# Turning normalised tokens by DMA through DRAM and VectorE 32x32 blocks in a fused attention and gate kernel

## The chip, the cores and the metric

The kernel runs on one core of a Trainium2 chip. The metric is the device time of one execution in microseconds (us); lower is better. Times are medians of several runs of the same program. A second source is one execution recorded by the hardware profiler; its span runs from the first instruction to the last.

The engines of the core: TensorE (PE in the profile; PEld is its weight load), VectorE (DVE), ScalarE (ACT), GpSimd (POOL), and SyncE (SP), which here only issues DMAs. Each engine works through its own instructions in order, and so does each queue of DMA issues: an instruction that waits holds up all behind it on its engine.

## The reference

Eight batches of 1024 tokens with 512 features, 16 heads of 32 features, all in float32:

```python
xn = layernorm(x)                      # mean and variance over the 512 features
q, k, v = (split_heads(xn @ W.T + b) for W, b in ((Wq, bq), (Wk, bk), (Wv, bv)))
scores = q @ k.T / sqrt(32)
im = arange(1024) % 256
scores = where(im[:, None] >= im[None, :], scores, -1e30)
s = merge_heads(softmax(scores) @ v) @ Wo.T + bo
y = clip((xn @ sign(ffn_weights).T) * scale + bias, -100, 100)
out = x + s * (y * sigmoid(y))
```

The mask depends on the positions modulo 256 only. The attention result and the gate both start from the layer-normalised tokens `xn`, and both need `xn` with features on partitions, because a matmul sums over partitions.

## The kernel before, in words

**Tiling.** The tokens of a batch are cut into eight tiles of 128 (`tokens`, `load_x`). A tile holds 32 tokens from each of the four windows of 256, so that the mask becomes causal between tiles and only the tiles on the diagonal need a mask inside. Four tiles make a half (512 tokens). The features are four chunks of 128 (`NC`), and one chunk is one group of four heads.

**The loop.** The loop from line 1109 goes over 8 batches x 4 groups x 9 steps. In each step:

- `probs_quad` makes scores with keys on partitions, four heads side by side, in one PSUM tile of four banks (the "t" quad, L592, L603, L614). ScalarE takes the exponential out of it (L627).
- `attend_quad` multiplies the step before's probabilities with the values (L640).
- `maxima_quad` makes scores of the next group with queries on partitions (the "s" quad, L525), and VectorE takes their row maxima (L537). They become the shifts of the next group's exponentials (`shift_parts`, L551, `shift_rows`).
- Between these, TensorE gets products of other parts: the query, key and value projections, the gate product (`gate_work`, L456, followed by VectorE's L433, L434, L442 and a store, L445), and the output product of the batch before (`output_work`, L739, L740, L741, a store, L742).

The pool `ps_q` has one buffer, so the two quads of a step use the same four banks: the s quad waits until the exponential has read the t quad, and the next t quad waits until the maxima have been read.

**The planner.** Matmuls are emitted by hand in this order. `Beside` holds a list of `Work` items with a cost in us. `fill` takes items from it until their costs reach what the step wants: some 1.2 us between the t and the s quad, and 2.35 us or more after the s quad, or the group's even share. The order of the items is in strings (`OPENING` for batch 0, `STEADY`, `CLOSING` for the last batch), in which each word is one block. A free item (cost 0), such as an operation of VectorE or a DMA, hangs on a block by its number (`link`). It is emitted when that block comes up, if its `ready` says so. Otherwise it is put off. Free items that come up before the s quad are kept until the maxima have been emitted.

**Normalising the next batch.** The words `N0` and `N1` stand for the two halves of the next batch. Per tile there are: the statistics on VectorE (`stats`, L292, L293; marked late, at most two are emitted at the end of a step), a few small operations per half on GpSimd (`scale`), the normalised tile in place on ScalarE (`normalise`, L316), and the turn (L320 to L331): four TensorE transposes of 128x128 (L328) into a PSUM bank and a ScalarE copy to `xnT` (L329). The turn costs 0.5 in the planner and is marked `turn`, which keeps it to certain places in a step. Batch 0's own tiles are normalised and turned ahead of the loop, by the same function.

**The DMA queue.** Nearly all transfers are issued from SP: x tiles (`load_x`, L137), the gate's stores to DRAM and reloads (L445, L729), the second load of x for the residual (`xb`, L733), and the stores of the output (L742). The pool `xpool` has five buffers for x tiles. The next batch's tiles 0 to 3 are loaded during group 0. The loads of tiles 5, 6 and 7 are linked so that each comes after the turn of tile 0, 1 and 2.

Of the kernel before, what the change touches and what calls it, by code (L numbers as in the profile page):

```python
# [9 lines left out]
F32 = mybir.dt.float32  # L10
# [6 lines left out]
P = 128  # L17
B = 8
L = 1024
D = 512  # L20
# [4 lines left out]
NC = D // P  # L25
NH = P // DK
HALF = 512
# [10 lines left out]
MT = P // NW  # L38
# [35 lines left out]
def tile_gated_window_attention(  # L74
# [16 lines left out]
    nc = tc.nc  # L91
    PSUM = bass.MemoryType.PSUM

    def pool(name, bufs, **kw):
        return ctx.enter_context(tc.tile_pool(name=name, bufs=bufs, **kw))
# [4 lines left out]
    seq = pool("seq", 2)  # L100
# [7 lines left out]
    rows_p = pool("rows", 1)  # L108
    small = pool("small", 4)
    spill = pool("spill", 2, space=bass.MemoryType.DRAM)  # L110
    ps_q = pool("ps_q", 1, space=PSUM)
    ps_a = pool("ps_a", 2, space=PSUM)
    ps_t = pool("ps_t", 2, space=PSUM)
# [7 lines left out]
    def bank(name, dtype=F32, n=512):  # L121
        return ps_t.tile([P, n], dtype, tag="bank", name=name)
# [8 lines left out]
    xt = {}  # L131
# [37 lines left out]
    for name, src in (("fscale", fscale), ("fbias", fbias), ("bo", bo)):  # L169
        t = const.tile([P, D], F32, name=f"{name}_r")  # L170
# [61 lines left out]
    wT, turned = {}, set()  # L232
# [46 lines left out]
        return [lambda c=c: turn(c) for c in range(NC)]  # L279


    xnT, scaled, normed = {}, set(), set()

    def norm_work(b, half):
        its = range(4 * half, 4 * half + 4)
        mv, rstd, shift_by = {}, {}, {}

        def stats(i, it):
            if i == 0:
                mv[0] = small.tile([P, 4, 2], F32, tag="mv", name=f"mv_{b}_{half}")  # L290
            st = small.tile([P, 6], F32, tag="st", name=f"st_{b}_{it}")
            nc.vector.bn_stats(st, xt[b, it])  # L292
            nc.vector.bn_aggr(mv[0][:, i, :], st)  # L293

        def scale(lo=0, hi=4):
            if lo == 0:
                rstd[0] = small.tile([P, 4], F32, tag="rstd", name=f"rstd_{b}_{half}")
            r = rstd[0][:, lo:hi]
            nc.gpsimd.tensor_scalar(r, mv[0][:, lo:hi, 1], EPS, None, ALU.add)
            nc.gpsimd.tensor_tensor(r, r, neg_half[:, lo:hi], ALU.pow)  # L300
            if b == 0:
                return
            shift_by[0] = small.tile([P, 4], F32, tag="nmr", name=f"nmr_{b}_{half}")
            scaled.add((b, half))
            nc.gpsimd.tensor_tensor(shift_by[0], mv[0][:, :, 0], rstd[0], ALU.mult)
            nc.gpsimd.tensor_scalar(shift_by[0], shift_by[0], -1.0, None, ALU.mult)

        def normalise(i, it):
            x = xt[b, it]
            normed.add((b, it))  # L310
            if b == 0:
                nc.vector.tensor_scalar(
                    x, x, mv[0][:, i, 0:1], rstd[0][:, i : i + 1], ALU.subtract, ALU.mult
                )
                return
            nc.scalar.activation(  # L316
                x, x, AF.Identity, bias=shift_by[0][:, i : i + 1], scale=rstd[0][:, i : i + 1]
            )

        def turn(i, it):  # L320
            if (b, half) not in xnT:
                xnT[b, half] = seq.tile([P, NC, HALF], F32, tag="xnT", name=f"xnT_{b}_{half}")
            turned.add((b, it))
            ps = bank(f"xnT_ps_{b}_{it}")
            x = xt.pop((b, it))
            normed.discard((b, it))
            for c in range(NC):
                nc.tensor.transpose(ps[:, c * P : (c + 1) * P], x[:, c * P : (c + 1) * P], ident)  # L328
            nc.scalar.copy(  # L329
                xnT[b, half][:, :, i * P : (i + 1) * P], ps.rearrange("p (c t) -> p c t", c=NC)  # L330
            )  # L331

        return (
            [lambda i=i, it=it: stats(i, it) for i, it in enumerate(its)],
            scale,
            [lambda i=i, it=it: normalise(i, it) for i, it in enumerate(its)],
            [lambda i=i, it=it: turn(i, it) for i, it in enumerate(its)],
        )

    def xn_cols(b, it):  # L340
# [39 lines left out]
    def values_work(b, it):  # L380
        def after(ps):

            vt[b, it] = vpool.tile([P, D], F32, tag="v", name=f"v_{b}_{it}")
            nc.scalar.copy(vt[b, it], ps)

        return product(
            f"v_ps_{b}_{it}",
            [(lambda c=c: (xn_cols(b, it)[:, c, :], wT["wv"][:, c, :])) for c in range(NC)],
            0.86,
            after,  # L390
            lambda: (b, it) in turned,
        )

    def heads_work(b, g, half, which):

        w, bias, into = {"q": ("wq", bq_c, qt), "k": ("wk", bk_c, kt)}[which]

        def after(ps):
            if (b, g) not in into:
                into[b, g] = qk.tile([P, L], F32, tag=which, name=f"{which}_{b}_{g}")  # L400
            nc.scalar.activation(  # L401
                into[b, g][:, half * HALF : (half + 1) * HALF], ps, AF.Identity,
                bias=bias[:, g : g + 1], scale=1.0,
            )

        return product(
            f"{which}_ps_{b}_{g}_{half}",
            [
                (lambda c=c: (wT[w][:, c, g * P : (g + 1) * P], xnT[b, half][:, c, :]))
                for c in range(NC)  # L410
            ],
            0.86,
            after,
            lambda: all((b, half * 4 + i) in turned for i in range(4)),
        )
# [423 lines left out]
    def link(i, fn, tail=False):  # L839
        links.append((i, fn, tail))  # L840

    def plan(b, g, text):
        for word in text.split():
            kind, number = word[0], word.strip("'")[1:]
            bb = b + word.count("'")
            i = len(blocks)
            if kind == "|":
                for block in blocks:
                    block.early = block.early or block.at == (b, g)
                continue  # L850
            if kind == "N":
                half = int(number)
                stats, scale, normalise, turn = norm_work(b + 1, half)
                for k in range(4):
                    done = lambda key=(b + 1, 4 * half + k): key in normed
                    there = lambda key=(b + 1, 4 * half + k): key in xt
                    link(
                        i - 5 + (2 + k // 2 if half else 0) + k // 2,
                        Work(0, stats[k], late=True, ready=there),
                    )  # L860
                    by = lambda key=(b + 1, half): key in scaled
                    link(i + half + max(1, k), Work(0, normalise[k], ready=by))
                    link(i + half + 2 + k, Work(0.5, turn[k], turn=True, ready=done))
                link(i - 2 + 2 * half, Work(0, scale, late=True, ready=there))
                continue
            if kind == "-":
                main = []
            elif kind in "qk":
                main = heads_work(bb, int(number[0]), int(number[1]), kind)
            elif kind == "V":  # L870
                main = values_work(bb, int(number))
            elif kind == "W":
                main = [Work(0.5, turn_weight("wo")[int(number)], turn=True)]
            elif kind == "R":
                spread, main = row_work()
                link(i - 3, spread)
            elif kind == "O":
                fetch, main = output_work(b - 1, int(number))
                link(i - 1, fetch)
            else:  # L880
                split, main, squash, finish = gate_work(bb, int(number), kind == "H")
                if split is not None:
                    link(i - 3, split)
                later = 1 if b in (0, B - 1) else 0
                link(i + 2 + later, squash)
                link(i + 3 + later, finish)
            blocks.append(Block((b, g), main))

    for b in range(B):
        for g in range(NC):  # L890
# [7 lines left out]
            elif g == 1:  # L898
                for k in range(4):

                    ready = lambda key=(b + 1, k - 1): key[1] < 0 or key in turned
# [121 lines left out]


    norms = [norm_work(0, half) for half in range(2)]

    warm = ps_a.tile([P, 512], F32, tag="av", name="warm")

    def idle_turns(n):
        for _ in range(n):  # L1030
            nc.tensor.transpose(warm[:, 0:P], ident, ident)

    idle_turns(36)
    stats, scale, normalise, turn = norms[0]
    key_turns, first_keys = turn_weight("wk"), heads_work(0, 0, 0, "k")
    first_keys = [w.split(0.43) for w in first_keys]
    stats[0]()
# [30 lines left out]
    stats, scale = norms[1][:2]  # L1068
# [40 lines left out]
    for s, (b, g, n) in enumerate(steps):  # L1109
# [4 lines left out]
        turn = {0: (b, g, 0), 7: (*nxt, 1) if nxt else None}.get(n)  # L1114
        add = {LAST[1] + 2: None if last else (b, g, 1), 2: (*old, 0) if old else None}.get(n)
        now, kept = side(b, g), []
# [87 lines left out]
    b, g = B - 1, NC - 1  # L1204
# [66 lines left out]
```

## Time and profile before

| what | value |
|---|---|
| median of 3 runs | 2215.35 us (2215.28 to 2217.46) |
| span of the profiled execution | 2213.6 us, so 1.75 us of the median lie outside the span |
| TensorE busy | 2182.9 us, granted clock 1.000 |
| GpSimd busy | 1325.6 us |
| VectorE busy | 1276.7 us |
| ScalarE busy | 876.0 us |
| DMA | 93.60 MB, 42 GB/s over the span |

A step of the loop takes 6.9 to 8.3 us, a group of nine 64 to 69 us, a batch some 268 us. Batch 0 and the start before it are slower in places, and the last batch has no next batch beside it. TensorE is busy nearly all the time; the other engines wait for it. The profile gives busy time per group of instructions, what each waited for, and single instructions in a window of the timeline. A row of a group reads: line, engine, operation, output and inputs with their shapes, count, then the busy time and the mean of one in ns, then the idle time of the engine just before them and what ended it.

### The profile page before, as it was taken

To read this page: it belongs to the slowest core of one execution; us is meant where nothing else is said; L and a number is where in the kernel's file an instruction comes from. 1 tells how busy PE (TensorE), PEld (TensorE's weight loads), DVE (VectorE), ACT (ScalarE), POOL (GpSimd) and SP (SyncE) were. 2 spreads that over 40 slices of the span, in tenths; PEclk is the share of its full clock that TensorE was granted. 3 is DMA by queue.
4 is the path that set the end of the run, shared out by engine and by line. 5 is a ranking of instruction groups with operands and counts; after the bars stand their busy time and mean duration, and the time that the engine had idled before them with its cause. 6 is when DMAs were issued, how large, how long until landed. Compare 5 with 4: busy or idle time off the path is not lost. (4 is left out here: it accounts for less than half of the span.)

```text
span 2213.6 us, 57362 instructions
## 1 busy us (share of the span) xinstructions
PE 2182.9 (99%) x26015; PEld 857.3 (39%) x26015; DVE 1276.7 (58%) x1635; ACT 876.0 (40%) x862; POOL 1325.6 (60%) x1198
## 2 busy tenths in 40 slices
PE   8999999999999999999999999999999999999998
PEld 4334333333333443333333333334333443333333
DVE  4556556665557655566555665565655665555564
ACT  2235433444344444344443443434443343333332
POOL 1356565666566656576556665556765666755562
PEclk9999999999999999999999999999999999999999
DMA  4001000121001210012000120002200111000113
GB/s 167 2 16 35 11 7 30 54 73 35 25 25 40 73 35 25 25 59 72 16 25 25 63 68 16 25 25 68 63 16 25 45 59 63 11 21 25 44 54 125
DMA packets 49676, 93.60 MB, mean 42 GB/s; under 512 B 5388, under 2 KB 5656, under 8 KB 49432
## 3 DMA queue, kind: packets, MB, share of 16 engines
q1 hardware_dynamic: 48728, 88.76, 12.1%
q8 instruction: 203, 3.33, 0.6%
q10 hardware_dynamic: 704, 1.18, 0.2%
q14 instruction: 41, 0.34, 0.0%
HBM read 56.37 MB, written 33.55 MB: 41 GB/s over the span
## 5 line engine op out<-in xcount | busy, mean ns | idle before, releaser
L659 POOL TENSOR_TENSOR p<-p,p 128x512 f32<-128x512 f32 x930 | 1096.3, 1209 | 395.2 <-ACT p L627 242.9
L537 DVE TENSOR_REDUCE pm<-s 128x4 f32<-128x2048 f32 (+3 forms) x384 | 664.0, 1750 | 588.6 <-PE s L525 586.7
L627 ACT ACTIVATE p<-t 128x2048 f32<-128x2048 f32 x288 | 540.9, 1878 | 839.3 <-PE t L614 764.0
L715 DVE RECIPROCAL aT<-aT 128x128 f32<-128x128 f32 x256 | 230.3, 928 | 214.9 <-ACT aT L676 214.9
L525 PE MATMUL s<-k,q 32*128 32x512 f32 (+3 forms) x3072 | 315.3, 504 | 1.1 <-ACT q L401 0.8
L640 PE MATMUL av<-p,v 128*32 128x512 f32 (+3 forms) x3072 | 307.4, 495 | 1.6 <-DVE aT L719 1.4
L614 PE MATMUL t<-q,k 32*128 32x512 f32 (+3 forms) x3072 | 306.1, 492 | 0.0
L358 PE MATMUL k_ps<-xnT,wkT 128*32 128x512 f32 (+3 forms) x2832 | 254.9, 477 | 1.7 <-ACT wkT L274 0.7
L358 PE MATMUL q_ps<-xnT,wqT 128*32 128x512 f32 (+2 forms) x2656 | 254.1, 497 | 1.7 <-ACT shift L572 0.8
L358 PE MATMUL v_ps<-wvT,xnT 128*32 128x512 f32 (+3 forms) x2728 | 254.8, 489 | 0.0
L358 PE MATMUL o_ps<-woT,aT 128*32 128x320 f32 (+2 forms) x2568 | 243.9, 503 | 1.5 <-ACT shift L572 0.8
L741 POOL TENSOR_TENSOR s<-s,xb 128x512 f32<-128x512 f32 x63 | 86.3, 1370 | 212.3 <-DVE s L740 210.2
L358 PEld LDWEIGHTS k_ps<-xnT,wkT 128*32 128x32 f32 x2832 | 83.7, 109 | 169.0 <-issue 138.3
L614 PEld LDWEIGHTS t<-q,k 32*128 32x128 f32 x3072 | 139.1, 185 | 25.8
L358 PEld LDWEIGHTS q_ps<-xnT,wqT 128*32 128x32 f32 x2656 | 78.9, 109 | 174.0 <-issue 151.6
L640 PEld LDWEIGHTS av<-p,v 128*32 128x32 f32 x3072 | 70.3, 108 | 195.9 <-issue 163.4
L358 PEld LDWEIGHTS v_ps<-wvT,xnT 128*32 128x32 f32 x2728 | 79.2, 109 | 168.6 <-issue 143.5
L456 PE MATMUL y_ps<-fwT,x 128*128 128x512 f32 x464 | 135.5, 418 | 1.7 <-ACT k L401 1.3
L525 PEld LDWEIGHTS s<-k,q 32*128 32x128 f32 x3072 | 117.0, 184 | 52.0 <-ACT p L627 42.2
L358 PEld LDWEIGHTS o_ps<-woT,aT 128*32 128x32 f32 x2568 | 76.1, 109 | 151.4 <-issue 133.1
L429 POOL TENSOR_TENSOR x<-xnT,x 128x512 fp32r<-128x512 f32 x58 | 74.1, 1277 | 100.0 <-ACT x L428 100.0
L435 POOL TENSOR_SCALAR y<-y 128x512 f32<-128x512 f32 x64 | 39.6, 619 | 153.1 <-DVE y L434 101.3
(96 smaller groups left out, 1475.8 us busy)
## 6 DMA issues: line engine op xcount, KB each, us to landing
g<-t SPq DMA_DIRECT2D x64, 256.0 KB, 2.0
gb<-g SPq DMA_DIRECT2D x64, 256.0 KB, 2.9
xb<-in_L_attn_x_dram SPq DMA_DIRECT2D x64, 256.0 KB, 3.1
out_dram<-s SPq DMA_DIRECT2D x63, 256.0 KB, 2.5
x<-in_L_attn_x_dram SPq DMA_DIRECT2D x62, 256.0 KB, 3.1
wq_st<-in_L_attn_Wq_dram SPq DMA_DIRECT2D x2, 512.0 KB, 5.1
wv_st<-in_L_attn_Wv_dram SPq DMA_DIRECT2D x2, 512.0 KB
fw_st<-in_L_ffn_weights_dram SPq DMA_DIRECT2D x2, 512.0 KB, 9.7
```

The costliest lines, as they stand in the source:

```text
L358: nc.tensor.matmul(hold[0][cols, lo:hi], lhsT=lhsT[:, cols], rhs=rhs[:, lo:hi], start=(i == 0 and lo == 0), stop=(i == n - 1), skip_group_ ...
L429: nc.gpsimd.tensor_tensor(part[1], src, part[0].bitcast(F32), ALU.subtract)
L435: nc.gpsimd.tensor_scalar(y[0], y[0], MAX_VAL, -MAX_VAL, ALU.min, ALU.max)
L456: nc.tensor.matmul(hold[0], lhsT=part[i][:, c, :], rhs=wT["fw"][:, c, :], start=(i == 0 and c == 0), stop=(i == 1 and c == NC - 1),)
L525: nc.tensor.matmul(sc[:, h, at : at + w], lhsT=qt[b, g][head_rows(h), i * P : (i + 1) * P], rhs=kt[b, g][head_rows(h), lo:hi], start=(at = ...
L537: nc.vector.tensor_reduce(pm[:, 0 if lo == 0 else 1, i, :], sc[:, :, at : at + w], AX.X, ALU.max)
L614: nc.tensor.matmul(sc[:, h, at : at + w], lhsT=kt[b, g][head_rows(h), j * P : (j + 1) * P], rhs=qt[b, g][head_rows(h), q0 : q0 + w], start ...
L627: nc.scalar.activation(pt[:, :, :width], sc[:, :, :width], AF.Exp, scale=SCALE)
L640: nc.tensor.matmul(av[b, g, f][head_rows(h), lo : lo + w], lhsT=vt[b, j][:, g * P + h * DK : g * P + (h + 1) * DK], rhs=pts[b, g, n][:, h, ...
L659: nc.gpsimd.tensor_tensor(t[:, hs, lo : lo + w], t[:, hs, lo : lo + w], p[:, hs, at : at + w], ALU.add)
L715: nc.vector.reciprocal(r, r)
L741: nc.gpsimd.tensor_tensor(s, s, xr, ALU.add)
```

## The change

From the second batch on, the four transposes and the copy of a turn are replaced by two steps. Both are free items.

- `shuffle`, as soon as a tile is normalised: SP stores the tile of 128 tokens x 512 features (256 KB) to DRAM. Four DMAs load it back into the same SBUF tile, each one filling 32 partitions. Partition block j gets, for each chunk c and token block t, the 32 features of block j in chunk c: 32 partitions x 16 pieces of 32 features (128 bytes), 64 KB a load. The first load waits until the store has landed.
- `turn_blocks`: one VectorE transpose of 128 x 512, which turns each block of 32x32 in place of its own, from the x tile into `xnT`.

With blocks moved by the DMA and each block turned by VectorE, `xnT` holds what the TensorE transposes gave. The shuffle hangs on the block on which the normalise hangs. The block transpose hangs on block i + 4 + k for tile k of its half; the TensorE turn hung on i + half + 2 + k. A new pool `moved` has four DRAM buffers. Batch 0's own tiles are turned on TensorE as before.

For 7 batches of 8 tiles, 224 TensorE transposes and 56 ScalarE copies go; 56 stores, 224 loads and 56 VectorE transposes come.

```diff
@@ pools
     spill = pool("spill", 2, space=bass.MemoryType.DRAM)
+    moved = pool("moved", 4, space=bass.MemoryType.DRAM)
@@ norm_work(b, half)
+        def shuffle(i, it):
+            x = xt[b, it]
+            kept = moved.tile([P, D], F32, tag="xd", name=f"xd_{b}_{it}")
+            nc.sync.dma_start(kept, x)
+            from_rows = kept.rearrange("(t p) (c j f) -> j p c t f", p=MT, j=NH, f=MT)
+            for j in range(NH):
+                nc.sync.dma_start(
+                    x[j * MT : (j + 1) * MT, :].rearrange("p (c t f) -> p c t f", t=NH, f=MT),
+                    from_rows[j],
+                )
+            shuffled.add((b, it))
+
+        def turn_blocks(i, it):
+            if (b, half) not in xnT:
+                xnT[b, half] = seq.tile([P, NC, HALF], F32, tag="xnT", name=f"xnT_{b}_{half}")
+            turned.add((b, it))
+            x = xt.pop((b, it))
+            normed.discard((b, it))
+            nc.vector.transpose(xnT[b, half][:, :, i * P : (i + 1) * P], x)
@@ plan(b, g, text)
-                stats, scale, normalise, turn = norm_work(b + 1, half)
+                stats, scale, normalise, _, shuffle, turn = norm_work(b + 1, half)
@@
                     link(i + half + max(1, k), Work(0, normalise[k], ready=by))
-                    link(i + half + 2 + k, Work(0.5, turn[k], turn=True, ready=done))
+                    link(i + half + max(1, k), Work(0, shuffle[k], ready=done))
+                    there2 = lambda key=(b + 1, 4 * half + k): key in shuffled
+                    link(i + half + 4 - half + k, Work(0, turn[k], ready=there2))
```

More of the change, by code (lines that the diff above doesn't have):

```diff
@@ L279, in turn_weight @@
         return [lambda c=c: turn(c) for c in range(NC)]
-    xnT, scaled, normed = {}, set(), set()
+    xnT, scaled, normed, shuffled = {}, set(), set(), set()
     def norm_work(b, half):
@@ L337, in norm_work @@
             [lambda i=i, it=it: turn(i, it) for i, it in enumerate(its)],
+            [lambda i=i, it=it: shuffle(i, it) for i, it in enumerate(its)],
+            [lambda i=i, it=it: turn_blocks(i, it) for i, it in enumerate(its)],
         )
@@ L1033, in tile_gated_window_attention @@
     idle_turns(36)
-    stats, scale, normalise, turn = norms[0]
+    stats, scale, normalise, turn = norms[0][:4]
     key_turns, first_keys = turn_weight("wk"), heads_work(0, 0, 0, "k")
```

## The prediction

> **What bounds the kernel now.** I read, in this order, the page's first part (engines), the waits, the costliest groups with shapes kept apart, the DMA issues, then the timeline of batch 4, the middle of five near-equal batches. 0.2% (4.4 us) is about what a measurement of this kernel can tell from no change.
>
> The page:
> ```profile
> span 2213.6 us, 57362 instructions
> PE 2182.9 (99%) x26015; PEld 857.3 (39%) x26015; DVE 1276.7 (58%) x1635; ACT 876.0 (40%) x862; POOL 1325.6 (60%) x1198
> ```
> The waits, engine by engine:
> ```profile
> ACT p L627 <- PE t L614: 764.0, 261, 6.5
> DVE pm L537 <- PE s L525: 586.7, 195, 11.0
> PEld s L525 <- ACT p L627: 42.2, 97, 0.8
> PEld L592 <- DVE pm L537: 29.1, 62, 1.8
> ```
> TensorE is busy throughout and ACT and DVE wait for it. But a busy PE does not set every step: with one four-bank PSUM buffer for both quads, a step is the loop t quad, exp (L627, 1878 ns), s quad, maxima (L537, 2287 ns), next t. PE's waits inside that loop are short because products fill them. The distance from one exp to the next, read off the timeline, shows what filling costs (groups, batches and steps count from 0): in group 0 of batch 7, with nothing of a next batch beside it, the nine steps are 6.89, 6.92, 6.95, 7.03, 7.12, 7.37, 7.21, 7.09, 7.17 us. I take these as the bare loop. Batch 4's groups last 67.0, 68.8, 66.4 and 66.0 us against that row's 63.7.
>
> Of what the change touches, groups (count | busy, mean ns | idle before):
> ```profile
> L328 PE MATMUL xnT_ps<-ident,x 128*128 128x128 f32 x256 | 41.5, 286 | 3.3 <-DVE x L312 1.6 <-DVE y L434 1.0 <-ACT xnT L329 0.4
> L329 ACT COPY xnT<-xnT_ps 128x512 f32<-128x512 f32 x64 | 37.2, 585 | 86.0 <-PE xnT_ps L328 86.0
> L434 DVE TENSOR_TENSOR y<-y_ps,fbias_r 128x512 f32<-128x512 f32 x64 | 44.3, 692 | 2.6
> L442 DVE SCALAR_TENSOR_TENSOR t<-t,y 128x512 f32<-128x512 f32 x64 | 53.4, 836 | 0.0
> L292 DVE BATCH_NORM_STATS2 st<-x 128x6 f32<-128x512 f32 x64 | 43.1, 674 | 8.8 <-DMA x<-in_L_attn_x_dram 8.8
> ```
> The last row matters: statistics stand in DVE's order before a maximum, so a late x stalls the loop. The one place where DVE, not PE, already sets the step, batch 4, group 2, step 0 (start, duration):
> ```profile
> 1286.32 0.94 DVE L715 RECIPROCAL aT<-aT 128x128 f32<-128x128 f32 x1
> 1287.18 0.70 DVE L442 SCALAR_TENSOR_TENSOR t<-t,y 128x512 f32<-128x512 f32 x1
> 1287.81 1.75 DVE L715 RECIPROCAL aT<-aT 128x128 f32<-128x128 f32 x2
> 1289.58 2.29 DVE L537 TENSOR_REDUCE pm<-s 128x4 f32<-128x2048 f32 x1
> ```
> The reduction follows two reciprocals with no gap. And the queue, SP, in DMA rows (KB each, us to landing) and timeline:
> ```profile
> g<-t SPq DMA_DIRECT2D x64, 256.0 KB, 2.0
> x<-in_L_attn_x_dram SPq DMA_DIRECT2D x62, 256.0 KB, 3.1
> ```
> ```profile
> 1259.98 1.36 SPq L137 DMA_DIRECT2D x<-in_L_attn_x_dram  x2
> 1287.91 0.33 SPq L445 DMA_DIRECT2D g<-t  x1
> 1293.83 0.54 SPq L733 DMA_DIRECT2D xb<-in_L_attn_x_dram  x1
> ```
>
> **The change, part by part.**
>
> *1. TensorE loses 56 of 64 turns.* A merged run of four transposes shows 0.65-0.66 us, and 0.59 us pass to PE's next instruction, so 56 turns are 33-36 us of PE time. What returns is limited by the bare loop. In batch 4 the turns fall in group 1's steps 5 to 8 (7.62+7.94+7.92+8.31 = 31.8 us; bare 28.8, room 3.0, turns 2.5) and group 2's steps 3 to 7 (37.6; bare 35.8, room 1.8): 2.5 + 1.8 = 4.3 us a batch. Batches 2 to 6 give 21.5, batch 1 about 3.8, batch 0 (crowded otherwise) 1.9: **-27 us**, at most -36. The 56 copies (33 us) leave ACT, which waits 764 us for PE: nothing.
>
> *2. DVE gains 56 block transposes of 128x512.* None is in the trace. DVE's operations on that shape take 0.43 (L266, a copy) to 0.84 us (L442); I take 0.70, the cluster of the rows at 674 to 692. All 56 are 39 us, mostly in gaps before a maximum. Where gaps are short they push. They are free works, so they are emitted two or three blocks later than the PE turns were, and with PE work gone, blocks close earlier: the gate's L433/L434 of the last gate product slide too. Counting DVE's order between maxima, batch 4's group 2, step 0, has before its maximum: 5.03 us of work before; after, two transposes (1.4) and L433/L434 (1.4) more, 7.83. No gap covers it, so the maximum, the next t quad and everything on PE behind it come **2.8 us** later. Four batches (3 to 6) have this order, batch 2 about 2.1: **+13 us** (+9 to +14 by the transpose's bounds).
>
> *3. SP gains 56 stores of 256 KB and 224 loads of 64 KB in pieces of 128 bytes.* The first load waits on SP for the store's landing (2.0 us by `g`), and every later g, gb, xb, out and x DMA queues behind. A tile's chain is 0.33 (issue, as L445) + 2.0 + four load issues of I each, and 2.5-3.1 until the last has landed. I is unknown: 128 pieces take 0.33 (L445) to 0.54 (L733), the weights' 256 pieces 0.46 to 0.60. With 0.14 per further 128 pieces on the store's 0.33, 512 pieces take **0.75 us**. [...] At 0.75 a tile holds SP 5.3 us, less than a step.
>  What waits: x5, x6, x7 need buffers that the turns of x0, x1, x2 free, and their loads stand behind the shuffles. x5's statistics must be done before the maximum of group 1's step 8. Adding the chain from the normalise, they are in time up to I = 0.95. x7's load now stands behind an xb load that waits for L740; its statistics come before the maximum of group 2's step 1, 1.65 to 1.9 us late in batches 3 to 6: **+7 us** (0 if the load slips ahead, +12 if its landing is 4 us as in crowded loads).
>
> [...] Packets of 512 bytes took a median 27 ns in this trace and those of 2 KB 84 ns; nothing shows 128. [...]
>
> *4. Batch 0*, whose plan is tighter. Transposes of x4 and x5 stand before the maximum of group 2's step 3, x6 and x7 before step 4's. Shuffles of the half begin only after its normalise, about 5 us into that group; two tile chains of 5.3 and a landing put x5 5.5-6.3 us behind the maximum, then x7 about 3. The two crowded DVE steps (group 1 step 7, group 2 step 0) add 1.4 and 1.7. Against these, 1 or 2 are absorbed because PE then lags its own fill: **+11 us** (+6 to +20 with I's bounds).
>
> *5. Batch 1* builds batch 2 with statistics of x5 to x7 right before maxima; its chain ends within a microsecond of need at I = 0.75: **+1**, and other x, xb and gb loads shifted by up to one tile's hold: **+2**. Gate stores and outputs behind the shuffles: 0, their readers wait tens of microseconds; that cover goes when SP falls a step behind.
>
> Sum against the profiled execution: -27 + 13 + 7 + 11 + 1 + 2 = **+7** on a span of 2213.6. With 1.75 us between that span and the median of 2215.35, 2222.4; I say 2222.
>
> **Rivals.**
>
> *All hidden.* PE may run behind DVE in those steps so that the late maxima cost nothing, and x arrive in time. For: PE is 99% busy, DVE only 58%. Against: the gapless reduction at 1289.58. Then only part 1 remains, with perhaps 5 us of batch 0's: 2188, between 2179 (-36) and 2205.
>
> *SP becomes the bound* (same sign, larger). Above I = 0.95 each 0.25 us costs 16 loads x 0.25 = 4 us a batch on the way to x5's statistics, and the late half spoils the next products. At 1.25 about +6 in five batches, 2252; at 1.5 about +11 and more in batches 0 and 1, 2285. [...] Against: 256 pieces at 0.46.
>
> *DVE hardly pushed, no gain either.* If planned fill merely spreads over the steps so that none shrinks below 7.3 us, part 1 falls to about -13 while the crowded steps cost half: 2215-2219, within the bound.
>
> That the turns are not taken from PE can be left out: the code emits none after batch 0's own.
>
> **How the numbers follow.** My forecast (crowded DVE steps and late x, SP hidden) 0.42, its own range 2210 to 2240; all hidden 0.25; SP bound 0.25; nothing either way 0.08. Leaving out the lower part of all hidden and the far tail of SP bound, 8 in 10 lie in 2188 to 2280. Faster: all hidden plus 0.04 of mine, 0.29. Same: 0.08 plus 0.05 of mine, 0.13. The remaining 0.58 is slower.
>
> **What would show it.** L328 falls from 256 to 32 instructions, L329 from 64 to 8. The block transposes' row has a mean of 0.6 to 0.8 us; a mean over 0.9 breaks part 2. Each 64 KB load's issue on SP near 0.75; over 1.0 and the SP rival holds. In batches 3 to 6 the first maximum of group 2 starts right behind reciprocals, some 2.8 us later after its step began, and the one after it waits for DMA through L292: that row's 8.8 us should grow to some 15 to 25. Group 1's steps 5 to 8 shrink to about 7.2 each. In batch 0's group 2 DVE waits 5 us and more for a DMA of x. If waits for DMA do not grow, all hidden holds; the forecast fails most likely by I, which no row of before fixes.

## The result and the profile after

The changed kernel takes 2235.7 us (2232.5 to 2239.1) against 2215.3 us before: ratio 1.0088, 95% interval 1.0075 to 1.0101, so 0.9% slower. The forecast was 2222, slower, with 2188 to 2280 as its range. The sign and most of the mechanism held. The size did not: +20 us where the forecast had +7. The changed kernel's runs also spread over 7 us where those of before spread over 2.

The profiled execution took 2237.9 us. Its page, first part:

```profile
span 2236.0 us, 57562 instructions
PE 2166.6 (97%) x25903; PEld 847.5 (38%) x25903; DVE 1307.0 (58%) x1691; ACT 844.6 (38%) x806; POOL 1322.4 (59%) x1198
```

TensorE is busy 16.3 us less and the span is 22.4 us longer: it waits now. The waits of after (engine, line, what it waited for: us in total, times, longest) say for what:

```profile
ACT p L650 <- PE t L637: 857.4, 267, 11.0
DVE st L293 <- DMA x<-in_L_attn_x_dram: 56.7, 14, 6.8
PEld L615 <- DVE pm L560: 55.2, 81, 4.7
PE t L615 <- DVE pm L560: 43.2, 26, 5.5
DVE xnT L339 <- DMA x<-xd: 5.7, 2, 4.9
```

The t quad's wait for the maxima (L615, L592 before) rose from 4.2 to 43.2 us on PE itself and from 29.1 to 55.2 at its weight loads. VectorE's wait for a tile of x ahead of the statistics rose from 8.8 to 56.7 us. The prediction named that row and gave it 15 to 25.

The new instructions, by groups with shapes kept apart:

```profile
L339 DVE STREAM_TRANSPOSE xnT<-x 128x512 f32<-128x512 f32 x56 | 38.7, 692 | 14.2 <-DMA x<-xd 5.7 <-ACT x L451 4.6 <-ACT q L424 3.9
L349 PE MATMUL xnT_ps<-ident,x 128*128 128x128 f32 x32 | 4.8, 284 | 2.8 <-DVE x L313 2.1 <-ACT xnT L350 0.4 <-ACT q L424 0.2
```

and the answer of the trace for the shuffle's tile (duration in ns, min/median/max) shows SP's cost:

```profile
L327 SPq DMA_DIRECT2D x<-xd x224: 557/629/1533, 182.2 to 1887.8; - x112
L324 SPq DMA_DIRECT2D xd<-x x56: 319/566/1286, 179.9 to 1882.5; - x56
```

A block transpose takes 0.692 us (the forecast had 0.70). A load of 512 pieces costs SP 0.629 us (the forecast had 0.75). Both unknown prices came out at or under the forecast, and the kernel is still slower than forecast.

The distance from one exponential to the next, read off the timelines (to within 0.01 us), shows where. Batch 4, steps 0 to 8, in us:

| | group 1 | group 2 |
|---|---|---|
| before | 7.13 7.74 7.35 7.29 7.56 7.62 7.94 7.92 8.31 | 7.14 7.17 7.13 7.56 7.61 7.62 7.43 7.38 7.37 |
| after | 7.13 7.40 7.13 7.26 7.12 7.37 7.23 7.14 **11.46** | **8.29 8.76** 7.17 7.29 7.32 7.37 7.21 7.10 7.17 |

All steps but three are as long as before (within 0.04 us) or shorter, near the bare loop: the relief of TensorE is there. Three steps give it back. The first is on this timeline of VectorE (start, duration, idle before and its end):

```profile
1300.41 0.69 DVE L293 BATCH_NORM_STATS2 st<-x 128x6 f32<-128x512 f32 x1 [6.83 <-DMA x<-in_L_attn_x_dram]
...
1301.23 0.92 DVE L738 RECIPROCAL aT<-aT 128x128 f32<-128x128 f32 x1
1302.07 2.29 DVE L560 TENSOR_REDUCE pm<-s 128x4 f32<-128x512 f32 x2
```

VectorE stood still for 6.83 us for tile 5's load, with the maxima behind it. SP's timeline, from the first store of this half on, shows why the load was late:

```profile
1271.95 0.32 SPq L324 DMA_DIRECT2D xd<-x  x1
1274.00 2.67 SPq L327 DMA_DIRECT2D x<-xd  x4
1276.78 0.57 SPq L324 DMA_DIRECT2D xd<-x  x1
1280.17 2.60 SPq L327 DMA_DIRECT2D x<-xd  x4
1282.87 0.61 SPq L765 DMA_DIRECT2D out_dram<-s  x1
1283.52 0.60 SPq L138 DMA_DIRECT2D x<-in_L_attn_x_dram  x1
1284.22 0.54 SPq L324 DMA_DIRECT2D xd<-x  x1
1288.77 2.62 SPq L327 DMA_DIRECT2D x<-xd  x4
1291.49 0.57 SPq L324 DMA_DIRECT2D xd<-x  x1
1293.81 3.39 SPq L327 DMA_DIRECT2D x<-xd  x4
1297.30 0.59 SPq L138 DMA_DIRECT2D x<-in_L_attn_x_dram  x1
```

The load of tile 5 (L138, at 1297.30) is issued right behind the fourth shuffle. Ahead of it SP waited 4.0 us for the third store's landing (1284.76 to 1288.77), while tile 4's load of 256 KB, issued at 1283.52, was in flight, and 1.75 us for the fourth's. From 1287.0 to 1288.25 the DMA share is 0.06 to 0.13, one or two of the sixteen engines: the rest stood idle. The packet records have one packet of 16 KB there, of the queue that the profile calls "instruction", from 1284.9 on and 1.6 us long. Whether it has a part in the late landing is not shown.

By batches, the sum of step lengths of after less that of before is +12.5, +2.6, +3.5, +0.9, +1.8, +1.8, -0.5 and +0.1 us: more than half is batch 0.

### The profile page after: what moved, and what is told of

Read it like the earlier page. It is cut to its first block, busy times and chain, and to the rows that moved or that the text cites. A ratio compares the mean times of both kernels' runs of the same rounds, so it can differ in the third digit from the quotient of the medians.

```text
span 2236.0 us, 57562 instructions
## 1 busy us (share of the span) xinstructions
PE 2166.6 (97%) x25903; PEld 847.5 (38%) x25903; DVE 1307.0 (58%) x1691; ACT 844.6 (38%) x806; POOL 1322.4 (59%) x1198
## 5 line engine op out<-in xcount | busy, mean ns | idle before, releaser
L663 PE MATMUL av<-p,v 128*32 128x512 f32 (+3 forms) x3072 | 313.5, 504 | 1.6 <-DVE aT L742 1.4
L637 PE MATMUL t<-q,k 32*128 32x512 f32 (+3 forms) x3072 | 312.5, 500 | 0.0
L381 PE MATMUL o_ps<-woT,aT 128*32 128x512 f32 (+3 forms) x2720 | 246.9, 488 | 0.0
L615 PE MATMUL t<-shift,neg 3*128 3x512 bf16 (+3 forms) x1536 | 115.3, 331 | 47.4 <-DVE pm L560 43.2
L381 PEld LDWEIGHTS v_ps<-wvT,xnT 128*32 128x32 f32 x2744 | 80.2, 110 | 174.4 <-issue 152.5
L381 PEld LDWEIGHTS o_ps<-woT,aT 128*32 128x32 f32 x2720 | 81.7, 111 | 161.9 <-issue 140.4
```

Source lines behind the costliest of these rows:

```text
L381: nc.tensor.matmul(hold[0][cols, lo:hi], lhsT=lhsT[:, cols], rhs=rhs[:, lo:hi], start=(i == 0 and lo == 0), stop=(i == n - 1), skip_group_ ...
L615: nc.tensor.matmul(sc[:, h, at : at + w], lhsT=neg1[r, :], rhs=shift[b, g, f][r, lo : lo + w], start=(k == 0), stop=False, skip_group_chec ...
L637: nc.tensor.matmul(sc[:, h, at : at + w], lhsT=kt[b, g][head_rows(h), j * P : (j + 1) * P], rhs=qt[b, g][head_rows(h), q0 : q0 + w], start ...
L663: nc.tensor.matmul(av[b, g, f][head_rows(h), lo : lo + w], lhsT=vt[b, j][:, g * P + h * DK : g * P + (h + 1) * DK], rhs=pts[b, g, n][:, h, ...
```

## The experiments

Two theories for the lost time. *Late x*: loads of x behind the shuffles hold the statistics, these the maxima, these TensorE. *Crowded VectorE*: the transposes in front of maxima are the price.

**Parts of the change alone.** Each edit is against the changed kernel.

No shuffle DMAs:

```diff
         def shuffle(i, it):
-            (one store, four loads)
             shuffled.add((b, it))
```

> The shuffle's store and four loads are left out, the VectorE transposes stay, so the values in xnT are not the turned tokens; only SP's queue and its landings change. Late-x theory (the loads of x5 to x7 stand behind the shuffles on SP, their statistics hold the maxima, TensorE idles over 3 us and then runs at half clock): the DMA waits at L293 fall from 56.7 to about 9 us, the granted clock returns to 1.000 outside batch 0, and the time is 2190 to 2202, since the two transposes before group 2's first maximum still cost about 2.8 us in four batches. Crowded-VectorE theory (the transposes in front of maxima are the main price): 2215 to 2230.

Measured: 2208.4 us (2207.3 to 2209.6), ratio to before 0.9969 (0.9957 to 0.998). The shuffle's DMAs are worth 27 us. The profiled executions lie 30.7 us apart: 11.8 of it are batch 0's, where VectorE had waited for the shuffle's own loads, and 19.2 are those of batches 1 to 6. Step 8 of group 1, where batch 4's stall stands, takes 46.2 us over these six batches, from 65.5. The wait for x fell to 19.2 us, not to 9, and the time is above the expected range: late x is the largest loss, not all.

A ScalarE copy for the transpose:

```diff
-            nc.vector.transpose(xnT[b, half][:, :, i * P : (i + 1) * P], x)
+            nc.scalar.copy(xnT[b, half][:, :, i * P : (i + 1) * P], x.rearrange("p (c t) -> p c t", c=NC))
```

> The shuffle's DMAs stay; each VectorE transpose is replaced by a ScalarE copy of the tile into xnT (0.6 us, as the copy that the change removed), so xnT holds unturned blocks. Late-x theory: the DMA waits at L293 stay at 45 us or more, the clock stays below 0.995, the time is 2220 to 2230. Crowded-VectorE theory: 2195 to 2208.

Measured: 2240.1 us (2237.7 to 2245.9). Taking 38.7 us of work off VectorE gained nothing, because the wait for x (64.1 us here) ends last. It is even 4 us slower; the ScalarE copies now wait 16.9 us for the shuffle's loads. This run alone could also mean that the copies' waits cost what the transposes had cost. The run with the moved loads, further below, keeps the transposes and gains 24 us: crowded VectorE as the main price is out.

Both edits together:

> Both left out: no shuffle DMAs, and a ScalarE copy in place of the transpose (values not turned). What is left of the change is TensorE's relief alone and the planner's new order. The steps of after that no late maximum touches are 5 to 6 us a batch shorter than before, so both theories expect 2178 to 2190, clock 1.000. The forecast's term of -27 us would give 2188. If the time is above 2200, the relief was not there and both theories fall.

Measured: 2200.5 us (2199.6 to 2201.3). That is 8 us under the first of these runs: with no shuffle, the transposes do cost. But 2200.5 missed the expected 2178 to 2190, with no shuffle and no transpose in the kernel, and is even just over the 2200 at which the expectation gave up both theories. Its VectorE timeline in group 2 of batch 4 shows a part of what is missing:

```profile
1288.35 0.69 DVE L293 BATCH_NORM_STATS2 st<-x 128x6 f32<-128x512 f32 x1 [2.89 <-DMA x<-in_L_attn_x_dram]
...
1289.18 2.26 DVE L551 TENSOR_REDUCE pm<-s 128x4 f32<-128x2048 f32 x1
```

and its SP timeline what that load stood behind:

```profile
1284.68 0.54 SPq L747 DMA_DIRECT2D xb<-in_L_attn_x_dram  x1
1285.32 0.55 SPq L138 DMA_DIRECT2D x<-in_L_attn_x_dram  x1
```

Tile 7's load waits behind the residual's (`xb`), as the prediction had it. It takes neither the shuffle nor the transposes, only the planner's new order: step 1 of group 2 is 8.7 to 8.8 us in four batches, from 7.17 before.

**Moving what waits.** The loads of tiles 4 to 7 go to ScalarE's queue; all of the change stays:

```diff
-                    fn = lambda b=b, it=4 + k: load_x(b + 1, it)
+                    fn = lambda b=b, it=4 + k: load_x(b + 1, it, nc.scalar)
```

> The whole change, but tiles 4 to 7 of the next batch are loaded from ScalarE's queue, so their loads do not stand behind the shuffles; nothing is left out of the computation. Late-x theory: the waits at L293 fall from 56.7 to under 20 us, steps 8 of group 1 shrink from 10.3 to 13.4 us to about 8, batch 0 keeps its 12 us, and the time is 2205 to 2217. Crowded-VectorE theory: the time stays at 2228 or above.

Measured: 2212.1 us (2209.1 to 2214.8), ratio 0.9982 (0.9973 to 0.9992). One word turns 20 us slower into 3 us faster. The wait for x is 10.1 us, from 56.7. Batch 0 kept its 12.1 us, as expected. The row of this run:

```profile
DVE st L293 <- DMA x<-in_L_attn_x_dram: 10.1, 6, 4.7
```

The same load edit on the kernel before, as a control:

> The kernel before, with the loads of tiles 4 to 7 on ScalarE's queue and its TensorE turns kept; nothing is left out of the computation. A control: if the gain of the two edits above comes from the relief of TensorE, this one gains nothing, 2212 to 2218. If moving the loads is worth something by itself, it is below 2208, and the change's own worth is smaller by that much.

Measured: 2213.9 us (2213.2 to 2215.7), ratio 0.9993 (0.9984 to 1.0001). The move by itself is worth nothing that can be told from no change.

The load edit on the version without shuffle and transpose:

> No shuffle DMAs, a ScalarE copy in place of the transpose (values not turned), and tiles 4 to 7 loaded from ScalarE's queue: TensorE's relief with no wait for x left. The forecast's first term, -27 us, gives 2188 (2180 to 2193). The 2200 measured with the loads on SP held x7's load behind xb; if that is all that was missing, 2185 to 2193. If it stays at 2198 or more, the first term was too large.

Measured: 2189.5 us (2188.0 to 2190.6), 25.9 us under before. The forecast's first term was -27. Step 1 of group 2 is back at 7.14 us: what the run with the loads on SP had lost there was x7's load.

**Batch 0.** Batch 1's tokens are turned on TensorE as before:

```diff
+                    if b == 0:
+                        link(i + half + 2 + k, Work(0.5, by_pe[k], turn=True, ready=done))
+                        continue
                     link(i + half + max(1, k), Work(0, shuffle[k], ready=done))
```

> The change everywhere but in batch 0: batch 1's tokens are turned on TensorE as before, nothing is left out of the computation. The forecast's part 4 says that the tighter plan of batch 0 costs about 11 us against a gain of 1.9 there: 2224 to 2227, group 2 of batch 0 back at 68 us. If the late loads of batch 0 merely take the place of another wait, group 2 stays above 74 us and the time is 2232 or more.

Measured: 2231.8 us (2227.1 to 2235.4). In the profiled execution batch 0's steps are back to those of before (group 2: 68.2 us, from 80.2). But the median fell by 4 us only, against the 9 to 12 expected. The profiled execution is the fastest of the four, 10.8 us under the profiled one of the changed kernel, and even in it batch 4 lost 8.9 us to before where the changed kernel had lost 1.8. So x's wait varies from batch to batch; that it covers the gain in the slower three is likely and not shown. Both edits together tell more:

> Loads of tiles 4 to 7 from ScalarE's queue and batch 1's tokens turned on TensorE, both edits together; nothing is left out of the computation. If the two losses add, the time is the 2212 of the ScalarE loads less about 10: 2199 to 2205, faster than the kernel before. If they are one and the same loss, it stays at 2209 to 2215.

Measured: 2198.3 us (2193.4 to 2201.8), ratio 0.9913 (0.9896 to 0.9929). Once x is on time, batch 0 is worth its 14 us (2212.1 less 2198.3). The two losses are separate ones: batch 0 has its own, and it does not go away with x on time.

**SP's wait for the store.** The loads of a shuffle are emitted one block after its store:

```diff
+            stored[b, it] = kept
+        def fetch_blocks(i, it):
+            x, kept = xt[b, it], stored.pop((b, it))
...
+                    link(i + half + max(1, k) + 1, Work(0, fetch[k], ready=kept))
```

> The whole change, but the four loads of a shuffle are emitted one block after its store, so that SP does not stand waiting for the store's landing; nothing is left out of the computation. If what holds x5's load is SP's wait for the landings (2.0 us and up to 4.5 us each, 123.7 us in all), those waits fall below 60 us and the time falls to 2218 to 2229. If the four load issues (2.6 us) and the data themselves hold it, the time stays at 2232 or above.

Measured: 2261.9 us (2260.9 to 2265.7), 26 us slower than the change. SP's waits for the landings fell to 62.6 us, as that theory had it, and the time went the other way. Its SP timeline in batch 4:

```profile
1280.63 1.03 SPq L324 DMA_DIRECT2D xd<-x  x2
1290.68 0.60 SPq L770 DMA_DIRECT2D out_dram<-s  x1
1291.33 0.59 SPq L138 DMA_DIRECT2D x<-in_L_attn_x_dram  x1
1292.03 6.39 SPq L331 DMA_DIRECT2D x<-xd  x8
```

After the two stores SP stands 9 us for an output store (L770) that waits for GpSimd; the first two tiles' loads are now queued behind it, and tile 5's load behind them (its statistics waited 10.97 us). Waits of 2 to 4 us were exchanged for one of 9. So this run does not show what the landings alone cost.

**The clock.** In the changed kernel the granted clock is 0.991 on average. In the windows of batch 4 (from:to, length, busy time and instructions, granted clock, DMA share, GB/s), the stall and what follows:

```profile
1301.00:1301.50 0.50, 0.00 (x0) 1.00 0.47 156
...
1304.50:1305.00 0.50, 0.50 (x8) 0.59 0.00 0
1305.00:1305.50 0.50, 0.50 (x4) 0.50 0.00 0
...
1307.50:1308.00 0.50, 0.50 (x8) 0.50 0.00 0
1308.00:1308.50 0.50, 0.50 (x20) 0.99 0.01 4
```

and TensorE's timeline there:

```profile
1304.41 0.48 PE L615 MATMUL t<-shift,neg 3*128 3x512 bf16 x4 [3.46 <-DVE pm L560]
1304.68 1.93 PE L637 MATMUL t<-q,k 32*128 32x512 f32 x8
```

After 3.46 us without work TensorE ran at half clock for some 3.4 us, and the t quad's eight matmuls took 1.93 us; one step later the same eight took 1.04. Shorter stretches had the same: in batch 0 the granted clock fell to 0.50 around idle stretches of 2.54 us (work begins again at 221.70) and 2.51 us (295.14), for 3.4 us the first time and 6.8 the second.

Is it a price of its own? Sixteen matmuls of zeros keep TensorE at work in that place:

```diff
+        if (g, n) == (1, NQ - 1) and 0 < b < B - 1:
+            for _ in range(4):
+                for h in range(NH):
+                    nc.tensor.matmul(av[b, g, 0][head_rows(h), :], lhsT=zeros, rhs=wT["wq"][:, 0, :],
+                                     start=False, stop=False, skip_group_check=True)
```

> The whole change, and in batches 1 to 6 sixteen matmuls of zeros added to an accumulation (about 2.1 us at full clock) stand at the end of group 1's step 8, where TensorE idles 3.5 us and is then seen at half clock for 3.4 us. The result is unchanged by zeros. Clock theory (part of the loss is the half clock after a long idle, not the wait itself): no half clock in group 2 of batches 2 to 5, step 0 of group 2 shorter by 1 us or more, 2225 to 2231. Rival (the order of VectorE sets those steps, the clock only shows it): the clock recovers, the time stays at 2233 to 2240. If the zeros delay the path instead, it is above 2240.

Measured: 2241.3 us (2238.7 to 2249.4); the clock rose to 0.995. Step 0 of group 2 fell in batches 2 and 3 (8.99 to 7.63 and 8.85 to 7.59 us) and rose in 4 and 5 (8.29 and 8.15 to 9.22); in batch 4 the clock was 1.00 there. The total did not fall: it lies above the 2240 that the expectation had as the sign that the zeros delay the path. So a steadier clock brought no time back here, but the run does not show that the half clock is free: the zeros may cost what it gives, and x5's wait varies by more than a microsecond between runs. What it costs stays open.

**Toward a better version.** Tile 6 on SP, since on ScalarE's queue its load waits for a transpose in front of an exponential:

```diff
-load_x(b + 1, it, nc.scalar)
+load_x(b + 1, it, nc.sync if it == 6 else nc.scalar)
```

> Batch 1's tokens on TensorE, tiles 4, 5 and 7 loaded from ScalarE's queue, tile 6 from SP; nothing is left out of the computation. With all four on ScalarE's queue, the load of tile 6 waits there for the transpose of tile 1 in front of an exponential, which starts 1.8 us late in four batches. If that wait is on the path, step 8 of group 1 falls from 8.97 to about 7.1 us and the time from 2198 to 2188 to 2193. If something else holds the exponential, it stays at 2196 or more.

Measured: 2196.0 us (2194.8 to 2198.0), ratio 0.9913 (0.9899 to 0.9926). Step 8 fell from 8.97 to 7.01 us as expected, but step 0 of group 2 rose from 8.65 to 9.16: a part of the time moved on to the crowded VectorE step. The expected 2188 to 2193 was missed, and the ranges of this run and of the one with all four loads on ScalarE (2193.4 to 2201.8) overlap.

And tile 2's transpose one block later:

```diff
-link(i + half + 4 - half + k, Work(0, turn[k], ready=there2))
+link(i + 4 + k + (k == 2 and not half), Work(0, turn[k], ready=there2))
```

> The version with tile 6 on SP, and tile 2's VectorE transpose linked one block later, so that only one stands before group 2's first maximum; nothing is left out of the computation. If two transposes there still cost what the forecast's part 2 says, step 0 of group 2 shrinks by 0.7 us in four batches and the time is 2 to 5 us under the version without this edit. If the gap covers them once x is on time, there is no difference beyond 1.5 us.

Measured: 2195.8 us (2193.1 to 2196.2), ratio 0.991 (0.9896 to 0.9923). In the profile, step 0 of group 2 fell from 9.16 to 8.51 us in four batches, the 0.7 us expected; the medians are equal, so the worth is not shown. This is the version to keep: 0.9% faster than the kernel before.

## Why the prediction was right in sign and short in size

- **Part 1, TensorE's relief: -27 us.** Right. The run with nothing but the relief gives -25.9; in batches 2 to 6 it is 22.2 us, where the forecast had 21.5. That the totals agree this closely is in part luck: this run also holds the gate's slide of part 2, and in batch 0 it is 1.4 us slower than before instead of 1.9 faster. Part 1's way, which limits the gain by the bare loop rather than by the 33 to 36 us of removed work, was what made the number.
- **Part 2, crowded VectorE: +13.** The mechanism is there and the size somewhat too large: in batch 4's group 2, step 0, the reduction follows two reciprocals without a gap, in the timeline of after:

```profile
1306.49 0.65 DVE L339 STREAM_TRANSPOSE xnT<-x 128x512 f32<-128x512 f32 x1
1307.07 0.67 DVE L456 TENSOR_TENSOR y_ps<-y_ps,fscale_r 128x512 f32<-128x512 f32 x1
1307.77 0.69 DVE L457 TENSOR_TENSOR y<-y_ps,fbias_r 128x512 f32<-128x512 f32 x1
1308.38 0.70 DVE L339 STREAM_TRANSPOSE xnT<-x 128x512 f32<-128x512 f32 x1
1309.01 0.70 DVE L465 SCALAR_TENSOR_TENSOR t<-t,y 128x512 f32<-128x512 f32 x1
1309.63 1.75 DVE L738 RECIPROCAL aT<-aT 128x128 f32<-128x128 f32 x2
1311.30 2.22 DVE L560 TENSOR_REDUCE pm<-s 128x4 f32<-128x2048 f32 x1
```

  Both transposes and the gate's two operations stand there, as worked out. With no shuffle this step takes 9.15 us, from 7.14 before: 2.0 us more where the forecast had 2.8, and over batches 2 to 6 some 10 us where it had 13. The transposes are 1.3 of it (7.88 without them), the gate's slide 0.7, which is there in the relief run too (7.87). Over the whole kernel the transposes' share measured 8 us (2208.4 less 2200.5) with no shuffle. With late x it cannot be added: without the transposes the time did not fall.
- **Part 3, x7 behind xb: +7.** Right, and by the wait that it named: step 1 of group 2 is 6.8 us longer over batches 3 to 6 (9.06, 8.76, 9.03 and 8.61 us, from 7.17 or 7.18). The planner's order does it even without a shuffle. Freeing the loads there was worth 11 us in all (2200.5 less 2189.5), 6.3 of it in these four batches and 4.8 in batch 1.
- **Part 3, x5: "in time up to I = 0.95".** This is the step that failed. I was 0.63 and x5 was late all the same: in batch 4 VectorE waited 6.8 us for it. The chain of the four tiles held SP for 25.3 us (1271.95 to 1297.20 on the timeline of the result). From the start of a store to the first load behind it passed 2.05, 3.39, 4.55 and 2.32 us, 12.3 together, where the forecast had 4 times 2.33, 9.3: it took the landing as 2.0, and the landings that the trace gives have a median of 2.5 and reach 4.4. The sixteen load issues made 11.3 us, under the forecast's 12.0. The output store and tile 4's load in between took another 1.45, which the chain of the prediction does not have. And the time for all this was shorter than forecast. The prediction had only the timeline of before to take its deadline from; the first normalise and the exponential of group 1's step 8 there, and then after, are

```profile
1249.95 1.50 ACT L316 ACTIVATE x<-x,nmr,rstd 128x512 f32<-128x512 f32 x2
1278.11 1.88 ACT L627 ACTIVATE p<-t 128x2048 f32<-128x2048 f32 x1 [1.75 <-PE t L614]
...
1271.12 1.51 ACT L317 ACTIVATE x<-x,nmr,rstd 128x512 f32<-128x512 f32 x2
1295.21 1.88 ACT L650 ACTIVATE p<-t 128x2048 f32<-128x2048 f32 x1 [4.45 <-PE t L637]
```

  28.2 us before and 24.1 after. Of the 4.1 us between them 2.7 are the relief of part 1 (group 1's steps 0 to 7 last 60.5 us before and 57.8 after), and 1.3 a first normalise that comes later in the group. The gain of one part had become the loss of another, and the forecast had counted them as independent. How much each of these made of the delay no run separates. The price, nothing in the forecast, was some 19 us: step 8 of group 1 over batches 1 to 6, against the run without the shuffle. That is more than the 13 us that the sum missed; the terms overlap and cannot simply be added. The SP rival had the right queue and not the whole price: the load issues were cheaper than forecast, and SP's waits for the landings took 10.3 of the 25.3 us.
- **Part 4, batch 0: +11.** Right within its range: batch 0 is 12.5 us longer, the edit there is worth 14 once x is on time. No run shows the bounds of I that this part's range goes by; the load issues of after took 0.557 to 1.533 us, with 0.629 as their median. Its VectorE waited 4.86 us for a shuffle's load, as foreseen ("5 us and more"). But 2.9 us of it, step 0 of group 2 at 11.2 us, is there in the relief run too (11.0): TensorE waits there for the gate's product on VectorE, which slid in the new order, and neither transpose nor shuffle has a part in it. The two rows of after:

```profile
221.70 0.41 PE L589 MATMUL mT_ps<-identb,mt 128*32 128x128 bf16 x16 [2.54 <-DVE y L457]
251.80 0.71 DVE L339 STREAM_TRANSPOSE xnT<-x 128x512 f32<-128x512 f32 x1 [4.86 <-DMA x<-xd]
```

- **The pieces of 128 bytes.** No packet of before shows that size. A line through its medians, 27 ns for 512 bytes and 84 ns for 2 KB, gives some 13 ns, an estimate, and so about 0.4 us for a load's 512 pieces on 16 engines. In the packet records of after, 114688 packets of 128 bytes took a median 13 ns and those of 2 KB 84 ns. A byte costs two and a half times as much in the small ones, and 512 of them over 16 engines are 0.42 us, as the line gave.

## What to carry to other kernels

When an edit frees the engine that bounds a loop, redo every deadline with the shorter steps: a transfer that was in time on the old timeline can be late on the new one, as tile 5's was here in batch 4, where VectorE waited 6.83 us for it. On a DMA queue that issues in order, as SP's did here (tile 5's load went out at 1297.30, right behind the fourth shuffle), ask of each new transfer what is queued behind it and of each delayed one what it slips behind; here the same shuffle came to +20 or -3 us against before by the place of loads that are no part of it, and to +46 by the place of its own. Free the loads first, then judge the edit: its other costs can be covered while one wait ends last, as the transposes' were here (2240.1 us with ScalarE copies in their place, 2235.7 with them).

## What was not expected of the hardware

- TensorE's granted clock fell to 0.50 at idle stretches of 2.5, 3.5 and 5.5 us, for 3.4 or 6.8 us, and the mean to 0.991; keeping TensorE busy brought it to 0.995 and gained no time.
- The issue of a DMA of 512 pieces held SP for 0.63 us, hardly more than that of a load of 128 pieces (0.54 to 0.60): the pieces' number is not what an issue costs here.
- A shuffle's store of 256 KB took from 2.0 to 4.4 us to land where the trace gives the landing, and SP's longest wait for one was 4.7.
